# Four convolution layers on one core: the Fourier layer's modes kept with channels innermost, and the order of buffers at the start of layer 2

## The chip, the core and the metric

The kernel runs on one core of a Trainium2 chip. The core has TensorE (PE: matmuls; PEld: its weight loads), VectorE (DVE), ScalarE (ACT), GpSimd (POOL) and SyncE (SP, which here only issues transfers), a working memory SBUF of 128 partitions, the accumulators PSUM that matmuls write, and 16 DMA engines to the main memory. The metric is the device time of one execution in microseconds (us). A profile is one execution recorded instruction by instruction; its lines name the lines of the kernel file ("L1286" is line 1286).

The kernel is written in a language in which the programmer states operations on tiles, and the compiler adds the waits, picks buffers from pools and orders each engine's instructions. Inside a block `with tc.manual_schedule(...)` the order of the named engines is that of the text. Layers 0 to 2 have such a block around their main loop; layer 3 has none, nor have the lines ahead of the loop in layer 2.

## What is computed

The input x is 4 images of 64 channels and 256 x 256 points, all in 32-bit floats. Four layers follow one another; each adds to x a function of its group-normalized x:

```python
x = x + L0(gn(x))   # 1x1 conv, 8x8 patch FFT filter, depthwise 3x3, gated gelu, 1x1 conv
x = x + L1(gn(x))   # 3x3 conv
x = x + L2(gn(x))   # 3x3 neighbourhood differences select one of two 1x1 convs
x = x + L3(gn(x))   # Fourier layer

def gn(v, G=32, eps=1e-5):            # 32 groups of 2 channels, over a whole image
    return (v - mean) / sqrt(var + eps)

def L3(x, w1, w2):                    # M1 = M2 = 16 modes
    x_ft = rfft2(x)
    top = einsum('bixy,ioxy->boxy', x_ft[:, :, :16, :16], w1)
    bot = einsum('bixy,ioxy->boxy', x_ft[:, :, 256-16:, :16], w2)
    out_ft = zeros; out_ft[:, :, :16, :16] = top; out_ft[:, :, 256-16:, :16] = bot
    return irfft2(out_ft, s=(256, 256))
```

Only 32 x 16 of the Fourier modes are used, so layer 3 is done with small DFT matrices: along the rows' direction (h), then along w, then the product with the modes' weights, then back.

## The kernel before: the parts that the change touches

Three large buffers named slots are shared by all layers; each has two copies. A new tile in a slot takes the copy that becomes free:

```python
self.slots = tc.tile_pool(name="slot", bufs=2)
def slot(self, k, name):
    return self.slots.tile([128, 11, self.W + 2], F32, tag=f"y{k}", name=name)
```

Layer 1 loads its rows into slots 0 and 1 by turns (n is one of 64 steps), normalizes them on ScalarE into two tiles of slot 2, and has in its loop:

```python
xns = [self.slot(2, f"xn1_{k}")[:, 0:10] for k in range(2)]
...
x = xt[n] = self.slot(n % 2, f"x1_{n}")[:, 0:10, 0:W]        # load
...
for n in range(NI):                    # NI = 64, manual schedule
    load(n + 3)
    product(n, 1)                      # L852: matmuls
    fetch(n)                           # L860: ScalarE, s<-m
    product(n, 2)
    finish(n - 1)                      # ScalarE sums, store
    transform(n + 1, 1, 2)             # L842: VectorE, reads xn
    middle(n)                          # L866: VectorE, s<-s,m
    product(n, 0); result(n, 0)        # L872
    transform(n + 1, 0, 3)
    normalize(n + 2)                   # L256: ScalarE, xn<-x
    product(n, 3); result(n, 3)
```

Layer 2 begins with (L954 is the memset, L967 the load's transfer, L1004 that of r, L147 and L981 small constants):

```python
xns = [self.slot(k, f"xn2_{k}_{i}")[:, 0:10] for i, k in enumerate((1, 2, 2))]
z = p_z.tile([128, 2, 10, W + 2], F32, name="z")
for t in xns + [z[:, 0], z[:, 1]]:
    nc.gpsimd.memset(t[:, :, 0 : W + 2 : W1], 0.0)
...
def load(n, g, s, ins=None):           # step n, half g, side s
    if s == 0:
        xt[n, g] = self.slot(((2 * n + g) % 3) % 2, f"x2_{n}_{g}")[:, 0:10, 0:W]
    ... nc.sync.dma_start(...)
for n, g in ((0, 0), (0, 1), (1, 0)):
    for s in range(2):
        load(n, g, s)
...                                    # constants
with tc.manual_schedule(...):
    for g in range(2):
        normalize(0, g)                # L256: xn (2n+g) % 3 <- x (n, g)
    convolve(0)                        # L1082
    ...                                # L1038 differ, L1052 divergence
    load(1, 1, 0); load(1, 1, 1)
    load_r(0, 0, 0); ...
```

Layer 3, forward half. There are B = 4 images; a group is CC = 4 channels of one image, 1 MB, so 16 groups per image; x has six buffers (three slots of two). NW = NH = 2, M = 16, C = 64:

```python
for b in range(B):
    ah = p_ah.tile([128, NW, C, 4 * M], F32, tag="ah", name=f"ah_{b}")     # one buffer
    for c0 in range(0, C, CC):
        x = ...load(b, c0, ...)                            # L1217
        for c1 in range(0, CC, 4):
            ps = ps_a.tile([128, 2, W], F32, tag="a")      # two buffers
            for n in range(NH):
                for j in range(2):
                    nc.tensor.matmul(ps[halves[j]], eh[:, n, :],           # L1258: along h
                                     x[:, c1 + 2*j : c1 + 2*j + 2, n, :], ...)
            m = p_a.tile([128, 2, W], F32, tag="m")        # three buffers
            nc.scalar.copy(m, ps)                          # L1263
            pt = ps_t.tile([128, NW, 2, 2, 4 * M], F32, tag="t")           # two buffers
            for n in range(NW):
                for k in range(2):
                    nc.tensor.transpose(...pt[:, n, k]..., m[:, k, ...], self.ident)   # L1267
            for n in range(NW):
                nc.vector.tensor_copy(                     # L1273
                    ah[:, n, c : c + 4, :].rearrange("p (j k) f -> p k j f", j=2), pt[:, n])
    if b < 3:
        load_w(b * NK)                                     # 2 MB of weights

    psx = ps_x.tile([128, 4, 128], F32, tag="x")
    ahv = ah.rearrange("p n c (s g k r) -> p n g r k s c", s=2, g=4, k=4)
    for n in range(NW):
        for ri in range(2):
            for g in range(4):
                nc.tensor.matmul(psx[32*g : 32*g + 32]..., ew[:, n, ri, :], ahv[:, n, g, ri],
                                 ..., tile_position=(0, 32 * g))           # L1286: along w
    xw = p_a.tile([128, 4, 128], F32, tag="m")
    nc.scalar.copy(xw, psx)                                # L1293

    pxt = ps_x.tile([128, 2, 4, 4, 2, M], F32, tag="xt")
    for s in range(2):
        for k in range(4):
            for h in halves:
                nc.tensor.matmul(pxt[h, s, k]..., xw[:, k, s*C : (s+1)*C], self.ident, ...)   # L1299
    for s in range(2):
        xb = xm[:, s, :, :, :, b].rearrange("p (g k) w r -> p k g w r", g=4)
        for k in range(4):
            v = pxt[:, s, k].rearrange("p g r w -> p g w r")
            nc.vector.tensor_scalar(xb[up, k], v[up], r[up], None, ALU.mult)               # L1309
            nc.vector.tensor_scalar(xb[low, k, :, :, 0], v[low, :, :, 1], r[low], -1.0, ...)   # L1310
            nc.vector.tensor_scalar(xb[low, k, :, :, 1], v[low, :, :, 0], r[low], ...)      # L1311
    ...                                                    # L1314: two tiny operations
```

After the loop come the product with the modes' weights (L1325, tile psm, out of xm), and the inverse half (L1350 to L1384), which loads x again, adds the result and stores it. A 32-bit matmul is two instructions in the trace, a transpose one.

Of the kernel before, what the change touches and what calls it, by code (L numbers as in the profile page):

```python
# [10 lines left out]
F32 = mybir.dt.float32  # L11
U32 = mybir.dt.uint32
AF = mybir.ActivationFunctionType
ALU = mybir.AluOpType
# [3 lines left out]
C = 64  # L18
# [100 lines left out]
class _Net:  # L119
# [812 lines left out]
    def _layer2(self, ctx, src, dst):  # L932
        tc, nc, a, B, H, W = self.tc, self.nc, self.a, self.B, self.H, self.W
# [13 lines left out]
        W1 = W + 1  # L947
        halves = [slice(0, C), slice(C, 128)]
        quarters = [slice(k * Q, (k + 1) * Q) for k in range(4)]

        xns = [self.slot(k, f"xn2_{k}_{i}")[:, 0:10] for i, k in enumerate((1, 2, 2))]
        z = p_z.tile([128, 2, 10, W + 2], F32, name="z")
        for t in xns + [z[:, 0], z[:, 1]]:
            nc.gpsimd.memset(t[:, :, 0 : W + 2 : W1], 0.0)  # L954
        its = [(b, r0) for b in range(B) for r0 in range(0, H, 32)]
        NI = len(its)
        xt, xn, rt, q, masks, sels, po, bst = ({} for _ in range(8))

        def load(n, g, s, ins=None):
            if n >= NI:  # L960
                return
            b, r0 = its[n]
            if s == 0:
                xt[n, g] = self.slot(((2 * n + g) % 3) % 2, f"x2_{n}_{g}")[:, 0:10, 0:W]
            top = r0 + 16 * g + 8 * s - 1
            i0, i1 = max(0, -top), min(10, H - top)
            d = nc.sync.dma_start(xt[n, g][halves[s], i0:i1], src[b][:, top + i0 : top + i1, :])  # L967
            if ins:
                self.after(d, ins)

        for n, g in ((0, 0), (0, 1), (1, 0)):
            for s in range(2):
                load(n, g, s)
        ones = cp.tile([128, Q], F32, name="ones")
        nc.vector.memset(ones, 1.0)
        peri, thr, scl = self.load("peri", cp), self.load("thr", cp), self.load("scl", cp)
# [225 lines left out]
    def _layer3(self, ctx, src, dst):  # L1202
        tc, nc, a, B, H, W = self.tc, self.nc, self.a, self.B, self.H, self.W
        pool = lambda c, name, bufs, **k: c.enter_context(tc.tile_pool(name=name, bufs=bufs, **k))
        M = MODES
        NH, NW = H // 128, W // 128
        CC, NK = 4, 2
# [17 lines left out]
        eh = self.load("c_eh", cp)  # L1225
# [10 lines left out]
        with ExitStack() as c2:  # L1236
            p_w = pool(c2, "l3w", 3)
            p_ah, p_a = pool(c2, "l3ah", 1), pool(c2, "l3a", 3)
            ps_a, ps_t = pool(c2, "l3pa", 2, space=PSUM), pool(c2, "l3pt", 2, space=PSUM)
            ps_x, ps_m = pool(c2, "l3px", 1, space=PSUM), pool(c2, "l3pm", 1, space=PSUM)  # L1240
            wts, xs = {}, {}
            self.small = lambda name: ps_m.tile([128, 512], F32, tag="m", name=name)

            def load_w(k0):
                wt = wts[k0] = p_w.tile([128, 2, NK, M * C], F32, tag="w", name=f"wt_{k0}")
                nc.sync.dma_start(wt, a["wf"][:, :, k0 : k0 + NK])

            for b in range(B):

                ah = p_ah.tile([128, NW, C, 4 * M], F32, tag="ah", name=f"ah_{b}")  # L1250
                for c0 in range(0, C, CC):
                    x = first.pop(c0, None) if b == 0 else None
                    x = xs[b, c0] = x or load(b, c0, f"x3_{b}_{c0}")
                    for c1 in range(0, CC, 4):
                        ps = ps_a.tile([128, 2, W], F32, tag="a", name=f"psa_{b}_{c0}_{c1}")
                        for n in range(NH):
                            for j in range(2):
                                nc.tensor.matmul(  # L1258
                                    ps[halves[j]], eh[:, n, :], x[:, c1 + 2 * j : c1 + 2 * j + 2, n, :],
                                    start=(n == 0), stop=(n == NH - 1),  # L1260
                                )
                        m = p_a.tile([128, 2, W], F32, tag="m", name=f"a_{b}_{c0}_{c1}")
                        nc.scalar.copy(m, ps)  # L1263
                        pt = ps_t.tile([128, NW, 2, 2, 4 * M], F32, tag="t", name=f"psat_{b}_{c0}_{c1}")
                        for n in range(NW):
                            for k in range(2):
                                nc.tensor.transpose(  # L1267
                                    pt[:, n, k].rearrange("p j f -> p (j f)"),
                                    m[:, k, n * 128 : (n + 1) * 128], self.ident,
                                )  # L1270
                        c = c0 + c1
                        for n in range(NW):
                            nc.vector.tensor_copy(  # L1273
                                ah[:, n, c : c + 4, :].rearrange("p (j k) f -> p k j f", j=2), pt[:, n]
                            )
                    if c0 % 16 == 0:
                        self.next_norms()
                if b < 3:
                    load_w(b * NK)

                psx = ps_x.tile([128, 4, 128], F32, tag="x", name=f"psx_{b}")
                ahv = ah.rearrange("p n c (s g k r) -> p n g r k s c", s=2, g=4, k=4)
                for n in range(NW):
                    for ri in range(2):
                        for g in range(4):
                            nc.tensor.matmul(  # L1286
                                psx[32 * g : 32 * g + 32].rearrange("p k (s c) -> p k s c", s=2),
                                ew[:, n, ri, :], ahv[:, n, g, ri],
                                start=(n == 0 and ri == 0), stop=(n == NW - 1 and ri == 1),
                                tile_position=(0, 32 * g),  # L1290
                            )
                xw = p_a.tile([128, 4, 128], F32, tag="m", name=f"xw_{b}")
                nc.scalar.copy(xw, psx)  # L1293

                pxt = ps_x.tile([128, 2, 4, 4, 2, M], F32, tag="xt", name=f"psxt_{b}")
                for s in range(2):
                    for k in range(4):
                        for h in halves:
                            nc.tensor.matmul(  # L1299
                                pxt[h, s, k].rearrange("p g r w -> p (g r w)"), xw[:, k, s * C : (s + 1) * C],  # L1300
                                self.ident, start=True, stop=True,
                            )
                r, nb = self.r[3][:, b : b + 1], self.nb[3][:, b : b + 1]
                up, low = halves
                for s in range(2):
                    xb = xm[:, s, :, :, :, b].rearrange("p (g k) w r -> p k g w r", g=4)
                    for k in range(4):
                        v = pxt[:, s, k].rearrange("p g r w -> p g w r")
                        nc.vector.tensor_scalar(xb[up, k], v[up], r[up], None, ALU.mult)  # L1309
                        nc.vector.tensor_scalar(xb[low, k, :, :, 0], v[low, :, :, 1], r[low], -1.0, ALU.mult, ALU.mult)  # L1310
                        nc.vector.tensor_scalar(xb[low, k, :, :, 1], v[low, :, :, 0], r[low], None, ALU.mult)  # L1311
                for k, h in enumerate(halves):
                    dc = xm[h, 0, 0, 0, k, b : b + 1]
                    nc.vector.scalar_tensor_tensor(dc, nb[h], float(H * W), dc, ALU.mult, ALU.add)  # L1314

            for k0 in range(0, M, NK):
                if k0 + 2 * NK < M and k0 > 0:
                    load_w(k0 + 2 * NK)
                wt = wts[k0]
                ps = ps_a.tile([128, 2, W], F32, tag="a", name=f"psm_{k0}").rearrange("p k w -> p (k w)")  # L1320
                ps = ps[:, 0 : NK * M * 2 * B].rearrange("p (k w r b) -> p k w r b", k=NK, w=M, r=2)
                for k in range(NK):
                    for kw in range(M):
                        for s in range(2):
                            nc.tensor.matmul(  # L1325
                                ps[halves[s], k, kw].rearrange("p r b -> p (r b)"),
                                wt[:, s, k, kw * C : (kw + 1) * C],
                                xm[:, s, k0 + k, kw].rearrange("p r b -> p (r b)"), start=True, stop=True,
                            )
                for k in range(NK):  # L1330
                    nc.scalar.copy(om[:, :, :, 0:2, k0 + k], ps[:, k].rearrange("p w r b -> p w b r"))
                    nc.vector.tensor_scalar(om[:, :, :, 2, k0 + k], ps[:, k, :, 0, :], -1.0, None, ALU.mult)
# [84 lines left out]
```

## Time and profile before

The median of three runs is 7476.2 us (7473.46 to 7483.11). The profiled execution has a span of 7469.9 us and a mean granted TensorE clock of 0.97.

| engine | busy us | share of the span | instructions |
|---|---|---|---|
| PE | 7164.3 | 96% | 188280 |
| PEld | 4283.8 | 57% | 188280 |
| DVE | 6440.8 | 86% | 5705 |
| ACT | 3917.9 | 52% | 4173 |
| POOL | 658.6 | 9% | 1435 |

Layer 0 takes the span up to about 4830 us, layer 1 to about 5525, layer 2 to about 6830, layer 3 the rest, of which the forward half goes to 7093, the product with the modes' weights to 7149 and the inverse half to the end.

How to read the lines that follow. A line of groups gives engine, operation, what it writes and reads, shape and count; then busy time and the mean of one in ns; then the engine's idle time before it and what ended most of that. A line of waits reads "who <- on whom: total us, times, longest us". In a timeline, a line begins with its start and its length in us; successive instructions of a kind are merged (x8), so that an instruction's own length is not always to be seen; the bracket is the idle time before it. Matmuls overlap, so the mean of one matmul is longer than the distance from one to the next. The share of DMA is the mean busy share of the 16 DMA engines; it can come out slightly over 1.

### The profile page before, as it was taken

The numbers are of one execution on the slowest core, as the hardware profiler recorded it, in microseconds if no ns is written. First come the engines' busy times: TensorE is split into PE (matmuls) and PEld (weight loads), VectorE is DVE, ScalarE is ACT, GpSimd is POOL, SyncE is SP. The second block draws the span as 40 slices with busy tenths as digits, with TensorE's granted clock in tenths as the row PEclk, the third lists the DMA queues.
The fourth block names the chain that finished last, engine by engine and source line by source line (L and its number), as shares of the span: only waits on it lengthen the run. The fifth ranks groups of instructions, "written<-read, shape, count | busy, mean of one in ns | idle before, by whom it ended". The sixth has DMA issues, their size and how long they took to land. (4 is left out here: it accounts for less than half of the span.)

```text
span 7469.9 us, 396764 instructions
## 1 busy us (share of the span) xinstructions
PE 7164.3 (96%) x188280; PEld 4283.8 (57%) x188280; DVE 6440.8 (86%) x5705; ACT 3917.9 (52%) x4173; POOL 658.6 (9%) x1435
## 2 busy tenths in 40 slices
PE   6999999999999999999999999899989999998797
PEld 4666666666666666666666666533334444443275
DVE  7999999999999999999999999889979889885345
ACT  3444444444554444454445445377768877773111
POOL 0000000000000000000000000011102222221011
PEclk9999999999999999999999999999999999999955
DMA  3222222222222222222111111399967666667689
GB/s 131 63 64 63 62 63 61 59 63 62 60 62 60 60 63 63 60 61 57 46 46 47 47 46 48 76 223 228 229 149 181 172 178 175 172 173 235 239 350 393
DMA packets 651193, 875.49 MB, mean 117 GB/s; under 512 B 44020, under 2 KB 470212, under 8 KB 647524
## 3 DMA queue, kind: packets, MB, share of 16 engines
q1 hardware_dynamic: 568548, 581.61, 29.0%
q0 software_dynamic: 81024, 268.50, 12.4%
q8 instruction: 1477, 24.20, 1.4%
q14 instruction: 144, 1.18, 0.1%
HBM read 581.50 MB, written 268.44 MB: 114 GB/s over the span
## 5 line engine op out<-in xcount | busy, mean ns | idle before, releaser
L482 PE MATMUL psd<-y,diag 32*32 32x512 f32 x73296 | 2526.3, 597 | 8.0 <-issue 7.6
L520 DVE SCALAR_TENSOR_TENSOR v<-y,sb_w_dw,v 128x2048 f32<-128x2048 f32 x1024 | 2391.5, 2335 | 112.3 <-ACT v L518 89.3
L482 PEld LDWEIGHTS psd<-y,diag 32*32 32x32 f32 x73296 | 1534.6, 103 | 837.3 <-issue 309.9
L462 ACT COPY y<-psy 128x512 f32<-128x512 f32 x1536 | 916.8, 661 | 1671.0 <-PE psy L455 1669.6
L420 DVE TENSOR_TENSOR up<-psu,flt 128x768 f32<-128x768 f32 x1024 | 933.0, 952 | 210.0 <-PE psu L417 209.5
L455 PEld LDWEIGHTS psy<-sb_c_bdft,up 64*64 64x64 f32 x49152 | 855.2, 135 | 340.4 <-issue 127.0
L455 PE MATMUL psy<-sb_c_bdft,up 64*64 64x64 f32 x49152 | 925.0, 221 | 22.8 <-issue 19.5
L417 PE MATMUL psu<-win,xf 64*64 64x384 f32 x8192 | 788.5, 489 | 23.3 <-DVE h L502 10.5
L1038 DVE TENSOR_TENSOR q<-xn 128x2313 f32<-128x2313 f32 (+2 forms) x256 | 628.0, 2496 | 1.7 <-ACT xn L256 1.7
L1093 PE MATMUL one<-z,wp 32*32 32x512 f32 x16384 | 594.6, 597 | 17.6 <-issue 13.1
L1039 ACT ACTIVATE q<-q 128x2313 f32<-128x2313 f32 (+2 forms) x256 | 529.1, 2086 | 32.2 <-DVE q L1038 30.9
L496 ACT ACTIVATE h<-psd 128x1024 f32<-128x1024 f32 x258 | 250.6, 1023 | 516.4 <-PE psd L482 516.4
L256 ACT ACTIVATE xn<-x,nb,r 128x1024 f32<-128x1024 f32 (+3 forms) x272 | 487.1, 1794 | 28.3 <-DMA x<-x 24.4
L1093 PEld LDWEIGHTS one<-z,wp 32*32 32x32 f32 x16384 | 366.9, 103 | 226.4 <-issue 84.6
L1052 PE MATMUL div<-q,ones 64*32 64x512 f32 x8192 | 468.6, 598 | 13.7 <-ACT q L1039 9.8
L427 POOL MEMSET y<- 128x22 f32 x384 | 51.8, 136 | 4212.2 <-ACT y L435 3204.1
L417 PEld LDWEIGHTS psu<-win,xf 64*64 64x64 f32 x8192 | 302.3, 135 | 193.1 <-issue 88.7
L1126 POOL DMA_DIRECT2D x<-r x512 | 273.5, 541 | 971.4 <-DVE r L1123 880.9
L852 PE MATMUL m<-t,wk 64*64 64x512 f32 x3072 | 341.1, 588 | 0.0
L1052 PEld LDWEIGHTS div<-q,ones 64*32 64x32 f32 x8192 | 154.1, 107 | 321.8 <-issue 257.8
L535 DVE TENSOR_TENSOR v<-g,v 64x1024 f32<-64x1024 f32 x257 | 313.5, 1220 | 9.3 <-ACT g L528 1.4
L502 DVE TENSOR_TENSOR h<-h,psd 128x1024 f32<-128x1024 f32 x258 | 302.7, 1215 | 6.1 <-PE psd L482 5.7
(154 smaller groups left out, 7403.2 us busy)
## 6 DMA issues: line engine op xcount, KB each, us to landing
x<-x SPq DMA_DIRECT2D x240, 640.0 KB, 6.6
x<-x SPq DMA_DIRECT2D x122, 1024.0 KB, 10.5
x<-in_x_dram SPq DMA_DIRECT2D x256, 256.0 KB, 3.7
x<-o POOLq DMA_DIRECT2D x128, 512.0 KB, 8.0
r<-x SPq DMA_DIRECT2D x512, 128.0 KB, 4.0
x<-r POOLq DMA_DIRECT2D x512, 128.0 KB, 3.8
out_dram<-x POOLq DMA_DIRECT2D x64, 1024.0 KB, 10.0
r<-in_x_dram SPq DMA_DIRECT2D x248, 256.0 KB, 3.8
```

The costliest lines, as they stand in the source:

```text
L256: self.nc.scalar.activation(dst, src, AF.Identity, bias=self.nb[n][p0:p1, b : b + 1], scale=self.r[n][p0:p1, b : b + 1])
L417: nc.tensor.matmul(ps[halves[n], s, 0:384], xf[t][halves[s], n, 4 * g + k], win[halves[s]], start=True, stop=True)
L420: nc.vector.tensor_mul(ups[t, g][:, :, k, :], ps[:, :, 0:384], flt.broadcast_to([128, 2, 384]))
L455: nc.tensor.matmul(ps[halves[c], n, s, :, k, :], up[halves[n], s, k, i * 128 + c * C : i * 128 + (c + 1) * C], bdft[halves[n]], start=True ...
L462: nc.scalar.copy(yt[t][i][:, 3:11, w0 : w0 + 64].rearrange("p r (k n w) -> p n r k w", k=4, n=2), ps[:, :, s])
L482: ins = nc.tensor.matmul(d[q // 2][quarters[j], q % 2], diag[quarters[q], i, k, :], rows_in(t, i, quarters[q], j, dy)[:, :, dx : dx + W], ...
L520: nc.vector.scalar_tensor_tensor(v, s, wdw[:, 2, k : k + 1], v, ALU.mult, ALU.add)
L852: nc.tensor.matmul(rows2(m)[halves[j], s], w[dx][halves[s]], ts[n][halves[s], i, 2 * j : 2 * j + 2, dx : dx + W], start=(dx == 0), stop=(d ...
L1038: nc.vector.tensor_sub(d, p0, p1)
L1039: nc.scalar.activation(d, d, AF.Square)
L1052: ins = nc.tensor.matmul(ps[quarters[j], h], ones[halves[h]], q[n, g, k][halves[h], r + 2 * j : r + 2 * j + 2, o : o + W], start=(m == 0), ...
L1093: ins = nc.tensor.matmul(rows2(ps[g])[quarters[j], k], w[quarters[i]], z[quarters[i], h, 2 * j + dy : 2 * j + dy + 2, dx : dx + W], tile_p ...
```

## The change

In layer 2 the first three loads are written ahead of the xn tiles, and xn takes its first two tiles from slot 2 and the third from slot 1; before, it took slot 1 first, and ahead of the loads. It is meant to give the first loads their buffers earlier.

In layer 3 the tile ah keeps the channels innermost, so that the matmuls along w read neighbours; PSUM tile pxt is laid out so that one VectorE operation covers all sixteen rows of modes, which makes 6 operations of 24 per image. The loop is written as steps over all 64 groups: step i has the matmuls of group i and the transposes of group i − 1, and an image's work along w follows one step after its last group.

```diff
-        xns = [self.slot(k, f"xn2_{k}_{i}")[:, 0:10] for i, k in enumerate((1, 2, 2))]
         z = p_z.tile([128, 2, 10, W + 2], F32, name="z")
-        for t in xns + [z[:, 0], z[:, 1]]:
-            nc.gpsimd.memset(t[:, :, 0 : W + 2 : W1], 0.0)
 ...
         for n, g in ((0, 0), (0, 1), (1, 0)):
             for s in range(2):
                 load(n, g, s)
+        xns = [self.slot(k, f"xn2_{i}")[:, 0:10] for i, k in enumerate((2, 2, 1))]
+        for t in xns + [z[:, 0], z[:, 1]]:
+            nc.gpsimd.memset(t[:, :, 0 : W + 2 : W1], 0.0)
 ... (layer 3)
+            ah_of = lambda b: ahs[b].rearrange("p n (s g k r) c -> p n g r k s c", s=2, g=4, k=4)
+            def along_h(b, c0):     # load, the matmuls of psa, ScalarE's copy: as before
+            def turned(b, c0):
+                if c0 == 0:
+                    ahs[b] = p_ah.tile([128, NW, 4 * M, C], F32, tag="ah", name=f"ah_{b}")
 ...                                  # the transposes as before
-                            nc.vector.tensor_copy(
-                                ah[:, n, c : c + 4, :].rearrange("p (j k) f -> p k j f", j=2), pt[:, n]
-                            )
+                    nc.vector.tensor_copy(
+                        ahs[b][:, n, :, c0 : c0 + 4].rearrange("p f (j k) -> p k j f", j=2), pt[:, n]
+                    )
+            def along_w(b):         # the matmuls of psx and ScalarE's copy, out of ah_of(b)
+            def spread(b):
-                pxt = ps_x.tile([128, 2, 4, 4, 2, M], F32, tag="xt", name=f"psxt_{b}")
+                pxt = ps_x.tile([128, 2, 4, 4, 2 * M], F32, tag="xt", name=f"psxt_{b}")
-                                pxt[h, s, k].rearrange("p g r w -> p (g r w)"), xw[:, k, s * C : (s + 1) * C],
-                                self.ident, start=True, stop=True,
+                                pxt[h, s, :, k], xw[:, k, s * C : (s + 1) * C], self.ident, start=True, stop=True
 ...
-                    xb = xm[:, s, :, :, :, b].rearrange("p (g k) w r -> p k g w r", g=4)
-                    for k in range(4):
-                        v = pxt[:, s, k].rearrange("p g r w -> p g w r")
-                        nc.vector.tensor_scalar(xb[up, k], v[up], r[up], None, ALU.mult)
-                        nc.vector.tensor_scalar(xb[low, k, :, :, 0], v[low, :, :, 1], r[low], -1.0, ALU.mult, ALU.mult)
-                        nc.vector.tensor_scalar(xb[low, k, :, :, 1], v[low, :, :, 0], r[low], None, ALU.mult)
+                    xb = xm[:, s, :, :, :, b]
+                    v = pxt[:, s].rearrange("p g k (r w) -> p (g k) w r", r=2)
+                    nc.vector.tensor_scalar(xb[up], v[up], r[up], None, ALU.mult)
+                    nc.vector.tensor_scalar(xb[low, :, :, 0], v[low, :, :, 1], r[low], -1.0, ALU.mult, ALU.mult)
+                    nc.vector.tensor_scalar(xb[low, :, :, 1], v[low, :, :, 0], r[low], None, ALU.mult)
 ...
+            groups = [(b, c0) for b in range(B) for c0 in range(0, C, CC)]
+            for i in range(len(groups) + 2):
+                if i < len(groups):
+                    along_h(*groups[i])
+                b, k = divmod(i - 1, NG)              # NG = 16 groups per image
+                if b > 0 and k == 0:
+                    along_w(b - 1)
+                if 0 < i <= len(groups):
+                    turned(*groups[i - 1])
+                if b > 0 and k == 0:
+                    spread(b - 1)
+                if i % NG == NG - 1 and i // NG < 3:
+                    load_w(i // NG * NK)
```

## The prediction

> **What bounds the kernel now.** I read the page first: TensorE is busy 96% of the span, so the time is TensorE's time plus its waits. The change touches two stretches only: the passage from layer 1 to layer 2 and the forward half of layer 3. So I asked each stretch for its own waits, groups and timeline.
>
> The passage, timeline between 5481 and 5512 us (start, length, engine, line, what; in brackets the idle time before it and who ended it):
>
> ```profile
> 5481.46 13.15 SPq L1004 DMA_DIRECT2D r<-x  x8
> ...
> 5487.58 2.79 ACT L256 ACTIVATE xn<-x,nb,r 64x256 f32<-64x256 f32 x2
> ...
> 5494.72 3.99 SPq L967 DMA_DIRECT2D x<-x  x2
> ...
> 5506.49 2.52 ACT L256 ACTIVATE xn<-x,nb,r 128x2560 f32<-128x2560 f32 x1 [16.12 <-DMA x<-x]
> 5508.92 1.09 ACT L860 ACTIVATE s<-m,i 128x1024 f32<-128x1024 f32 x1
> ...
> 5510.06 1.99 PE L852 MATMUL m<-t,wg 64*64 64x512 f32 x8 [9.57 <-ACT s L860]
> ```
>
> The ACTIVATE at 5506.49 is layer 2's: it normalizes rows (0,1), which the DMA of L967 fetches. That load was issued only at 5494.72, behind eight loads of r. ScalarE stands still for 16.12 us, and behind it in ScalarE's queue is L860, which belongs to layer 1. So TensorE idles 9.57 us inside layer 1.
>
> Why is the load late? Before takes layer 2's first xn from slot 1. Slot 1 has two buffers: the first one to fall free goes to xn (memset at 5469.54), the second is held by layer 1's last x until its normalization at 5487.58 has run its 2.79 us, to 5490.4.
>
> Layer 3, forward. The groups and waits between 6826 and 7100 us (groups: busy us, mean ns; then idle before; waits: total, times, longest):
>
> ```profile
> L1258 PE MATMUL psa<-x,sb_c_eh 128*64 128x512 f32 x512 | 130.1, 619 | 3.4 <-DVE r L1123 3.4
> L1273 DVE COPY ah<-psat 128x256 f32<-128x256 f32 x128 | 47.9, 420 | 131.2 <-PE psat L1267 130.9
> L1286 PE MATMUL psx<-ah,ew 128*32 128x512 f32 x128 | 28.2, 1034 | 1.0 <-DVE ah L1273 1.0
> L1309 DVE TENSOR_SCALAR xm<-psxt,r 64x128 f32<-64x128 f32 x32 | 14.2, 445 | 39.6 <-PE psxt L1299 39.1
> L1310 DVE TENSOR_SCALAR xm<-psxt,r 64x64 f32<-64x64 f32 x32 | 10.9, 340 | 0.5
> ```
> ```profile
> PE psat L1267 <- ACT a L1263: 42.9, 57, 1.8
> PE psm L1325 <- DVE xm L1314: 8.6, 1, 8.6
> ```
>
> Two things to see: psx streams 512 columns like psa, but takes 1034 ns against 619; and the transposes wait for ScalarE's copy in 57 of 64 groups. A steady group, from the timeline:
>
> ```profile
> 6851.72 0.66 PE L1267 MATMUL psat<-sb_c_ident,a 128*128 128x128 f32 x4 [0.72 <-ACT a L1263]
> 6852.31 1.94 PE L1258 MATMUL psa<-x,sb_c_eh 128*64 128x512 f32 x8
> 6854.33 0.58 ACT L1263 COPY a<-psa 128x512 f32<-128x512 f32 x1 [2.66 <-PE psa L1258]
> 6854.97 0.66 PE L1267 MATMUL psat<-sb_c_ident,a 128*128 128x128 f32 x4 [0.72 <-ACT a L1263]
> ```
>
> One group is 6854.97 − 6851.72 = 3.25 us. Last, windows of equal kind (length, busy of PE, PEld, DVE, ACT, POOL with counts, then granted clock, DMA share, GB/s):
>
> ```profile
> 6972.00:7011.00 39.00, 30.16 (x147) 11.26 (x146) 9.97 (x27) 7.02 (x12) 0.00 (x0) 1.00 1.02 362
> 7093.00:7149.00 56.00, 54.79 (x1024) 54.73 (x1024) 4.00 (x16) 6.04 (x16) 0.00 (x0) 0.50 0.49 190
> 7149.00:7470.00 321.00, 266.03 (x1408) 204.07 (x1408) 179.85 (x289) 38.68 (x64) 48.22 (x64) 0.56 1.01 399
> ```
>
> In the first the DMA engines are already full at 362 GB/s. The last two, the product with the modes' weights and the inverse half, are not edited; the inverse half is full of transfers (share 1.01).
>
> [...] psx reads elements 64 floats apart (256 bytes) and takes 1034 ns for 512 columns; psa reads neighbours and takes 619. [...] the trace has 0.50 all through the modes' product, which follows 8.6 us of waiting.
>
> **The change, part by part.**
>
> 1. Layer 2's first loads. Load (0,1) now gets the buffer of slot 1 that is free at 5469.5, and xn takes slot 2 for its first two tiles. The load can then land long before layer 1's tail needs ScalarE. The new waits are that xn tiles 0 and 1 need layer 1's own xn buffers: the trace shows the memset of the first at 5491.34, right after layer 1's VectorE work on it. They are waits on VectorE, not on a queue of transfers. I take back TensorE's 9.57 us, and nothing more, since everything after it in the passage hangs on layer 1's end: **−9.6 us**.
>
> 2. psx. With channels innermost its 64 channels are neighbours. Its 32 instructions run in four column groups, so eight steps; the trace has 7.06 us for them, 0.86 us a step. psa, with neighbours, has steps of 0.43 us (weight loads at 6856.03 and 6856.46). So 3.4 us, four times, all on TensorE: 4 × 3.5 = **−14 us**.
>
> 3. The 24 VectorE operations become 6. Before, the last run takes from 7084.49 to 7092.57, 8.1 us. From the two sizes in the groups the slope is (445 − 340)/64 = 1.64 ns per element; so 512 elements take 445 + 384 × 1.64 = 1075 ns and 256 take 340 + 192 × 1.64 = 655 ns. Two times (1075 + 2 × 655) = 4.8 us. Only the last of the four is on the path, the wait of psm: **−3.3 us**.
>
> 4. VectorE's copies into ah pay for it: their output now steps 256 bytes. Before shows what such a step costs elsewhere: ScalarE's L1373 takes 0.60 us for 256 elements with a stepped output, L1263 0.58 us for 512 without. [...] VectorE has 3.25 us per group: hidden, **0**.
>
> 5. The loop. Transposes of group i−1 are now written after the matmuls of group i, so ScalarE's copy could hide behind them. TensorE's own work for a group is 4 × 0.43 = 1.71 us plus 0.58 us of transposes = 2.29, so 0.96 us is to be had per group, 62 us at most. Two things cut it. First, transfers: a group is 1.05 MB, at 362 GB/s 2.90 us. Second, the layout of instructions. Layer 3 has no manual schedule, and the trace shows that the compiler reorders: after the first spread it placed 20 matmuls of psa (two and a half groups) between two sets of transposes (timeline at 6907.49), and at 6844.10 it placed ten, two of them of the next group. So matmuls that are ready move ahead of transposes, and transposes that are ready should likewise move ahead of matmuls whose x is not there. Up to group 37 the runs of matmuls straddle groups, and from 6981 on they do not: the compiler then took x to be late. In the new loop TensorE gets through its groups sooner, so the six loads in advance run out sooner. I guess the new order holds for some 15 groups and for a few after each of three spreads beyond those that already ran ahead, 20 in all: 20 × 0.96 = **−19 us**.
>
> 6. The modes' product and the inverse half: no edit, **0**. Weights are loaded three times in the forward half as before.
>
> Sum: −9.6 − 14 − 3.3 − 19 = −45.9, so 7476.2 − 45.9 = **7430.3 us**.
>
> **The rivals.** (a) The order is undone: the compiler puts each transpose straight after its copy as before. For: 57 waits of 64 in a kernel whose matmuls were free to move. Against: in the new text the matmuls stand first. Then only parts 1 to 3 count, −27, **7449 us**. (b) The order holds throughout and transfers take over as the bound. 58 groups of 1.05 MB and three weights of 2.1 MB are loaded in the forward half, 67 MB, of which about 6 are there by 6848 (18 us at 386 GB/s in that window, layer 2's last stores among them); 61 MB at 362 GB/s are 169 us, so the last x lands near 7017; about 13 us of transposes, psx and spread follow, and psm begins at 7030 instead of 7093. With part 1: −73, **7403 us**. (c) The wait of part 1 only moves: ScalarE now waits for slot 2 in the middle of layer 1. For: the first two xn do come later than before. Against: 5491 is still before the gap. It would take back up to 10 us: 7440. (d) The stepped copies become the bound of layer 3. They would have to exceed 1.6 us each, against 0.42 now: I give it almost nothing; it would cost about what the rest brings.
>
> **Range and chances.** (b) and (a) set the ends, widened by 5 us for the passage and for runs (7473 to 7483): 7398 to 7460. A gain of over 2% would need 150 us; all of layer 3's forward half is 263, and transfers keep 170 of it. A loss of 2% has no mechanism here that is large enough. Faster by over 2%: 0.02; within 2%: 0.97; slower: 0.01.
>
> **What would show it.** Right: no ScalarE wait on a transfer near 5490 to 5506 and TensorE without a gap there; psx near 600 ns; six TENSOR_SCALAR of 64x512 and 64x256 per batch near 1.1 and 0.65 us; the wait of psat on ScalarE down from 57 times to about 40. Wrong: psx still near 1 us (then the step was not the cause); copies into ah above 1.5 us; a forward half with the DMA share near 1 from end to end (then rival b); the inverse half longer, or its clock changed, which I hold fixed.

## The result, and the profile after

The changed kernel takes 7434.57 us (median, 7423.01 to 7437.48); the kernel before, in turns on the same chip, 7478.82 us. The ratio is 0.9938, 95% interval 0.9921 to 0.9956: 44 us less, where 45.9 were predicted.

Single profiled executions differ by more than a step is worth in stretches that nobody edited: layer 0, the same code in the same order, takes from 4837 to 4875 us in the profiles of this case. So each step is read in its own stretch, from starts and ends of matmuls in the trace. Stretches repeat better than totals: layer 3's forward half, where it is as before, takes 263.0 to 264.0 us in four profiles.

| stretch, us | before | after |
|---|---|---|
| layer 1, first to last matmul of m | 675.5 | 664.4 |
| gap of TensorE from there to the first psz of layer 2 | 10.4 | 10.6 |
| layer 2, first psz to first psa | 1297.8 | 1293.2 |
| layer 3 forward, first psa to first psm | 263.0 | 228.4 |
| psm to the end | 376.9 | 377.7 |

Two stretches carry the gain, 11.1 and 34.6 us. First the passage, timeline of the changed kernel (L964 is the load of x, L973 the memset of xn):

```profile
5480.55 26.49 SPq L964 DMA_DIRECT2D x<-x  x6
...
5502.29 0.13 POOL L973 MEMSET xn<- 128x20 f32 x1 [0.64 <-DVE t L842]
...
5502.46 2.94 ACT L256 ACTIVATE xn<-x,nb,r 64x256 f32<-64x256 f32 x2 [1.05 <-POOL xn L973]
...
5507.08 11.55 SPq L1004 DMA_DIRECT2D r<-x  x8
...
5512.75 2.52 ACT L256 ACTIVATE xn<-x,nb,r 128x2560 f32<-128x2560 f32 x1 [2.33 <-POOL xn L973]
```

The loads of x now stand ahead of the eight loads of r; before, the load of rows (0,1) stood behind them. ScalarE's two normalizations wait 1.05 and 2.33 us for the memset of their buffer, no longer 16.12 us for a transfer, and TensorE has no gap in layer 1.

Then layer 3, forward half: TensorE's waits, and the groups.

```profile
PE psat L1274 <- ACT a L1264: 27.6, 40, 2.0
...
PE psm L1346 <- DVE xm L1319: 5.2, 1, 5.2
```
```profile
L1278 DVE COPY ah<-psat 128x256 f32<-128x256 f32 x128 | 66.1, 601 | 120.4 <-PE psat L1274 120.3
...
L1290 PE MATMUL psx<-ah,ew 128*32 128x512 f32 x128 | 16.6, 597 | 1.4 <-DVE ah L1278 1.4
...
L1314 DVE TENSOR_SCALAR xm<-psxt,r 64x512 f32<-64x512 f32 x8 | 9.2, 1152 | 10.4 <-PE psxt L1306 10.3
```

psx has gone from 1034 to 597 ns a matmul and from 28.2 to 16.6 us in all, the copies into ah have gone from 420 to 601 ns, and the transposes wait for ScalarE in 40 groups instead of 57. Two of the four psx are not done in one go: the compiler puts the matmuls of a group's psa between their first 10 and their last 22 instructions, and such a psx takes 1.90 + 2.77 us, an undivided one 3.64:

```profile
6878.30 1.90 PE L1290 MATMUL psx<-ah,ew 128*32 128x512 f32 x10
...
6882.00 2.77 PE L1290 MATMUL psx<-ah,ew 128*32 128x512 f32 x22
...
6985.69 3.64 PE L1290 MATMUL psx<-ah,ew 128*32 128x512 f32 x32 [0.68 <-DVE ah L1278]
```

Timeline of the transposes, with the matmuls of psa left out: where the new order holds, a group takes 2.45 us (6847.24 − 6844.79); later in the same image the compiler puts a group's transposes right behind its copy again, and a group takes 3.27 us (6875.85 less 6872.58):

```profile
6844.79 0.66 PE L1274 MATMUL psat<-sb_c_ident,a 128*128 128x128 f32 x4
...
6847.24 0.66 PE L1274 MATMUL psat<-sb_c_ident,a 128*128 128x128 f32 x4
...
6872.58 0.66 PE L1274 MATMUL psat<-sb_c_ident,a 128*128 128x128 f32 x4 [0.16 <-ACT a L1264]
...
6875.85 0.66 PE L1274 MATMUL psat<-sb_c_ident,a 128*128 128x128 f32 x4 [0.74 <-ACT a L1264]
```

Windows: the first 30 us of steady work, the modes' product, and the inverse half. The last two are as before.

```profile
6842.00:6872.00 30.00, 30.00 (x148) 11.06 (x147) 12.60 (x24) 7.09 (x13) 0.00 (x0) 1.00 1.03 382
...
7054.00:7110.00 56.00, 54.79 (x1024) 54.70 (x1024) 4.05 (x16) 6.04 (x16) 0.00 (x0) 0.50 0.50 190
7110.00:7431.00 321.00, 269.12 (x1408) 208.12 (x1408) 180.00 (x289) 38.77 (x64) 48.24 (x64) 0.54 1.01 399
```

### The profile page after: what moved, and what is told of

It is laid out like the page before. It is cut to its first block, busy times and chain, and to the rows that moved or that the text cites. A ratio compares the mean times of both kernels' runs of the same rounds, so it can differ in the third digit from the quotient of the medians.

```text
span 7431.7 us, 396686 instructions
## 1 busy us (share of the span) xinstructions
PE 7153.8 (96%) x188280; PEld 4277.8 (58%) x188280; DVE 6445.5 (87%) x5633; ACT 3918.2 (53%) x4173; POOL 659.2 (9%) x1435
## 3 DMA queue, kind: packets, MB, share of 16 engines
q1 hardware_dynamic: 568548, 581.61, 29.3%
## 5 line engine op out<-in xcount | busy, mean ns | idle before, releaser
L417 PE MATMUL psu<-win,xf 64*64 64x384 f32 x8192 | 785.7, 488 | 22.3 <-DVE h L502 10.4
L1093 PE MATMUL one<-z,wp 32*32 32x512 f32 x16384 | 594.7, 599 | 15.5 <-issue 11.4
L256 ACT ACTIVATE xn<-x,nb,r 128x1024 f32<-128x1024 f32 (+3 forms) x272 | 487.1, 1794 | 15.3 <-DMA x<-x 8.3
```

The lines of the kernel that those rows point to most:

```text
L256: self.nc.scalar.activation(dst, src, AF.Identity, bias=self.nb[n][p0:p1, b : b + 1], scale=self.r[n][p0:p1, b : b + 1])
L417: nc.tensor.matmul(ps[halves[n], s, 0:384], xf[t][halves[s], n, 4 * g + k], win[halves[s]], start=True, stop=True)
L1093: ins = nc.tensor.matmul(rows2(ps[g])[quarters[j], k], w[quarters[i]], z[quarters[i], h, 2 * j + dy : 2 * j + dy + 2, dx : dx + W], tile_p ...
```

## The experiments

The theory: the passage gives 10 us, psx its own time, the spread's end 3 us, and the order of the loop the rest, in so far as the compiler keeps it. The rivals: the order counts for nothing, or transfers set the pace. A ratio below is to the kernel before on the same chip; "forward" is the stretch from the first psa to the first psm.

### One part alone: layer 2

```diff
 (before)
-        xns = [... for i, k in enumerate((1, 2, 2))]     # and their memsets, ahead of the loads
         ... the first three loads ...
+        xns = [... for i, k in enumerate((2, 2, 1))]     # and their memsets
```

> Before with the edit of layer 2 alone. If the gain there comes from the early load, layer 1 (first matmul on tile m to the last) shortens from 668 us by 9.6 to 11 us, TensorE's wait on ScalarE's s inside it is gone, and layer 3 stays as before (263 us from the first psa to the first psm). If the wait only moved to slot 2, layer 1 keeps a gap of 5 us or more and shortens by less than 5. Whole kernel about 10 us less; layer 0 is not edited, so a different layer 0 is run-to-run spread.

Measured: 7462.26 us, ratio 0.9976 (0.9966 to 0.9987). Layer 1's stretch falls from 675.5 to 665.1 us; forward is 263.4 us, as before. The wait was worth 10.4 us and is independent of layer 3.

### One part alone: the layout, in the loop of before

```diff
 (before)
-                ah = p_ah.tile([128, NW, C, 4 * M], F32, ...)
+                ah = p_ah.tile([128, NW, 4 * M, C], F32, ...)
-                    24 operations per image into xm
+                    6 operations per image into xm
```

> Before with the layout alone: channels innermost in ah, 6 VectorE operations of 24, the old order of the loop, layer 2 as before. My theory: the parts add, so the forward half of layer 3 shrinks from 263 us by 4 x 3.5 for psx and 3.3 for the last spread, to about 246; the wait of the transposes on ScalarE stays at 57 of 64. Rival: the layout made the loop overlap (VectorE gets free sooner), then it falls to 235 or less and the loop alone gives little.

Measured: 7457.2 us, ratio 0.9974 (0.9963 to 0.9985), forward 251.6 us: −11.4. An image's psx takes 3.64 us instead of 7.06, 13.7 for four, and the wait of psm 5.2 instead of 8.6. That would be 17, but the compiler orders the rest anew, and TensorE's waits now read:

```profile
PE psat L1267 <- ACT a L1263: 44.7, 61, 0.7
...
PE psat L1267 <- DMA x<-x: 3.2, 1, 3.2
```

That is 1.8 us more on ScalarE, and 3.2 us on a transfer at the start of layer 3 that before does not have. All of TensorE's waits in the stretch together are 1.2 us longer than before, in spite of the shorter wait of psm; with psx that makes −12.5 us, and TensorE's other matmuls take the 1.1 us more that are missing to −11.4. Near 246 us had been expected.

### One part alone: the loop, with the layout of before

```diff
 (the changed kernel)
-                    ahs[b] = p_ah.tile([128, NW, 4 * M, C], F32, ...)
+                    ahs[b] = p_ah.tile([128, NW, C, 4 * M], F32, ...)    # and 24 operations per image
 (and layer 2 as before)
```

> The new loop alone, with the old layout of ah, 24 VectorE operations, layer 2 as before. My theory: about 18 us off the forward half of layer 3 (263 to 245), psx still near 1030 ns, the wait on ScalarE down to about 40 of 64. Rival: the loop needs the shorter psx and spread to run ahead; then it gives under 8 us by itself.

Measured: 7466.01 us, ratio 0.9977 (0.9967 to 0.9988), forward 253.8 us: −9.2, between the theory's −18 and the rival's −8. The waits on ScalarE fall by 20.1 us, more than in the whole change, but other waits appear:

```profile
PE psat L1274 <- ACT a L1264: 22.8, 33, 1.0
...
PE psat L1274 <- DVE ah L1278: 5.3, 3, 2.7
```
```profile
L1290 PE MATMUL psx<-ah,ew 128*32 128x512 f32 x128 | 31.9, 1033 | 1.0 <-DVE ah L1278 1.0
```
```profile
7012.00:7022.00 10.00, 7.11 (x31) 2.19 (x27) 7.58 (x24) 1.39 (x3) 0.00 (x0) 0.90 0.84 297
7022.00:7032.00 10.00, 8.52 (x41) 3.23 (x39) 2.93 (x8) 1.75 (x3) 0.00 (x0) 0.93 0.80 259
```

With 2.8 us on transfers and the rest, TensorE's waits account for −13.8 us. Two things take part of it back. psx needs 31.9 us for 28.2, +3.7, because here too two of the four are cut by a group's psa. And around and after the last wait on VectorE the granted clock is 0.90 and 0.93 over 10 us each (the last two lines, windows; the clock stands third from the end), where it is 1.00 in the windows before and behind: from 7019.26 to 7023.99 TensorE takes 4.73 us for work of 3.05 (a group of 2.45 and four more transposes of 0.6), +1.7. That makes −8.4 of the −9.2. The parts don't add: −11.4 and −9.2 make −20.6, and together they bring −34.6. The wait of psat on VectorE's copies, 5.3 us here and absent with the new layout, is one reason, and the lower clock that was measured after it is another; the next experiments show both by themselves. The waits for a transfer, 3.2 us with the layout and 2.8 here, belong to neither part: the kernel with layer 2 alone has one of 2.5.

### The order held

```diff
 (the changed kernel)
+            with tc.manual_schedule(engines={mybir.EngineType.PE}):
                 for i in range(len(groups) + 2):
                     ... the loop, indented ...
```

> The changed kernel with TensorE's order in the forward loop of layer 3 held to that of the text, nothing else. If the compiler's order is what leaves 40 waits, these go, a group takes 2.45 us throughout while transfers keep up, and the forward half falls from 228 us to between 190 (TensorE's pace alone) and 203 (61 MB at 362 GB/s and the end): 25 to 38 us less than the changed kernel, with TensorE now waiting for x in some groups. Rival: the transfers are already the bound in the second stretch of 3.26 us (DMA share 0.99 there); then holding the order gives less than 8 us and the waits on ScalarE turn into waits on x.

Measured: 7398.43 us, ratio 0.989 (0.9876 to 0.9905), forward 199.1 us: 29.3 below the changed kernel, with the same instructions. Waits, and windows:

```profile
PE psat L1274 <- DMA x<-x: 7.7, 1, 7.7
...
PE psat L1274 <- ACT a L1264: 0.2, 1, 0.2
```
```profile
6842.00:6872.00 30.00, 29.89 (x152) 11.93 (x151) 13.35 (x32) 6.68 (x13) 1.09 (x2) 1.00 1.04 397
6890.00:6920.00 30.00, 30.00 (x149) 11.15 (x148) 14.74 (x30) 7.14 (x13) 0.00 (x0) 1.00 1.05 393
```

In these windows TensorE is busy in 29.89 and 30.00 of 30 us and the DMA engines are full too, at 397 and 393 GB/s (379 from 6930 to 6960): the two limits lie together, and x comes in time. All four psx are undivided. So the compiler's own order, not the transfers, kept the changed kernel at 228 us. The same kernel on another chip, with this expectation:

> The held order once more, beside the version with the early constants on the same chip. Ratio to before 0.989 as the first time, 0.9875 to 0.9905; forward half 197 to 202 us, gap at the start of layer 2 10.5 us.

gave 7406.38 us, ratio 0.9891 (0.9874 to 0.9907), forward 198.9 us, gap at the start of layer 2 10.4 us.

### The order held, with the old layout, and with the old loop

```diff
 (the order held)
-ahs[b] = p_ah.tile([128, NW, 4 * M, C], F32, ...)      # first: 24 operations and the old layout
+ahs[b] = p_ah.tile([128, NW, C, 4 * M], F32, ...)
 (the order held)
-for i in range(len(groups) + 2): ...                   # second: the loop of before,
+for b in range(B): for c0 in range(0, C, CC): ...      # the new layout
```

> The loop of the changed kernel with TensorE's order held, and the changed layer 2, but ah and pxt in the layout of before (24 VectorE operations, psx with a step of 256 bytes). Beside the held order with the new layout (forward half 199.1 us from the first psa to the first psm). Theory 'the gain of the layout is TensorE's own time and shows in full once the order is held': psx 1035 ns, 4 x 3.5 us more of psx and 3 to 7 us more in the last spread, forward half 213 to 222 us, total near 7415. Rival 'transfers set the pace, so psx hides behind them': only the last image's psx and spread show, forward half 203 to 209 us, total near 7404.

Measured: 7442.41 us, ratio 0.9934 (0.9915 to 0.9952), forward 228.4 us: 29.3 above the held order with the new layout, more than even the theory's upper end, and not hidden behind transfers. After an image's end, timeline of this kernel:

```profile
6959.94 2.32 DVE L1278 COPY ah<-psat 128x256 f32<-128x256 f32 x6
...
6960.84 0.63 PE L1274 MATMUL psat<-sb_c_ident,a 128*128 128x128 f32 x4 [2.80 <-DVE ah L1278]
```

and at the same place with the new layout:

```profile
6936.12 1.94 DVE L1278 COPY ah<-psat 128x256 f32<-128x256 f32 x4
...
6937.54 0.66 PE L1274 MATMUL psat<-sb_c_ident,a 128*128 128x128 f32 x4
```

The copies come after the 24 operations in VectorE's queue. These keep it from 6951.47 to 6959.94, 8.5 us, so the copies queue up (six in a row), both buffers of psat stay full, and TensorE waits 2.80 us; the six operations take 5.1 us (6931.04 to 6936.12) and end early enough. Such a wait comes at three boundaries, 8.4 us. After the first and the third TensorE's matmuls take nearly twice as long for a while:

```profile
6908.10 0.63 PE L1274 MATMUL psat<-sb_c_ident,a 128*128 128x128 f32 x4 [2.80 <-DVE ah L1278]
6908.66 3.61 PE L1259 MATMUL psa<-x,sb_c_eh 128*64 128x512 f32 x8
...
7011.91 1.09 PE L1274 MATMUL psat<-sb_c_ident,a 128*128 128x128 f32 x4 [2.81 <-DVE ah L1278]
...
7012.93 3.68 PE L1259 MATMUL psa<-x,sb_c_eh 128*64 128x512 f32 x8
```

Eight matmuls take 3.61 and 3.68 us for 1.94. At the first boundary a group takes 4.10 us for 2.45, at the third two groups up to 7019.64 take 7.73 us for 4.90: 1.7 and 2.8 us lost. With psx (13.7) and the last spread (3.4) that is 30.0 us; other waits are 0.5 us shorter, which leaves 29.5 for the 29.3 measured.

Not so after the second boundary, where the eight matmuls from 6961.40 on take 1.94 us. Windows of 10 us around each boundary, and the one after the third (PE's busy time stands second, the granted clock third from the end):

```profile
6904.00:6914.00 10.00, 7.20 (x30) 2.18 (x26) 6.02 (x19) 1.17 (x2) 0.00 (x0) 0.83 0.79 262
...
6954.00:6964.00 10.00, 7.20 (x38) 2.66 (x36) 7.97 (x26) 1.73 (x3) 0.00 (x0) 1.00 0.92 312
...
7004.00:7014.00 10.00, 7.19 (x34) 2.98 (x34) 8.96 (x29) 1.76 (x3) 0.00 (x0) 0.86 0.84 284
7014.00:7024.00 10.00, 10.00 (x42) 3.42 (x40) 2.27 (x6) 1.76 (x3) 0.00 (x0) 0.80 0.71 230
```

The three waits are equally long and TensorE is equally busy around them (7.20, 7.20 and 7.19 us), but the clock is 0.83 at the first, 1.00 at the second, and 0.86 and then 0.80 at the third. Why the second boundary keeps its clock is not shown.

> The new layout and the changed layer 2, but the loop of before (each group's transposes right after its copy, each image's psx and spread before the next image), with TensorE's order held as written. Theory 'ScalarE's copy on the path of every group is what the loop is about': 64 waits of psat on ScalarE of 0.72 us or more, 3.26 us per group, 64 x 3.26 = 209 us, and four psx and spreads of 8 to 11 us that nothing overlaps, forward half 240 to 252 us, total 7440 to 7450. Rival 'it is holding the order as such that brings the gain, whatever the order': forward half near 200 us.

Measured: 7476.61 us, ratio 0.9975 (0.9968 to 0.9982), forward 254.6 us, 55.5 above the new loop and 2.6 above the theory's range; one wait for a transfer at the layer's start takes 9.6 us. The line of waits on ScalarE is

```profile
PE psat L1268 <- ACT a L1264: 46.9, 63, 1.0
```

Holding an order brings nothing by itself (in the compiler's own order this loop takes 251.6 us); what is held must keep ScalarE's copy off TensorE's path.

### How many neighbours the matmul needs

```diff
 (the changed kernel; R = 4, then R = 2)
-ahs[b] = p_ah.tile([128, NW, 4 * M, C], F32, ...)
+ahs[b] = p_ah.tile([128, NW, C // R, 4 * M, R], F32, ...)   # psx: 16 steps of 256 columns for 8 of 512
```

> The changed kernel with ah cut so that 4 channels (16 bytes) are neighbours, and psx in 16 steps of 256 columns for 8 of 512. Theory [...] psx takes 3.4 us per image as with 64 neighbours; VectorE's copies [...] stay at 600 ns. Rival 'every step other than to the neighbour costs' : psx near 7 us per image. Rival 'it is the width of the step, 256 bytes': copies fall from 601 to about 420 ns. Total within 15 us of the changed kernel.

> The same with 2 channels (8 bytes) as neighbours. [...] psx between 3.4 us [...] and 5 us per image; copies [...] take between 420 and 600 ns. Rival 'every step costs': psx near 7 us. Total within 15 us of the changed kernel.

Measured: 7451.78 and 7439.52 us (one execution each; the kernel before takes 7497.27 on that chip), forward 228.2 and 229.0 us, as in the changed kernel. Groups, R = 4 first:

```profile
L1278 DVE COPY ah<-psat 128x256 f32<-128x256 f32 x128 | 68.6, 625 | 117.8 <-PE psat L1274 117.7
...
L1289 PE MATMUL psx<-ah,ew 128*32 128x256 f32 x256 | 15.9, 381 | 1.4 <-DVE ah L1278 1.4
```
```profile
L1278 DVE COPY ah<-psat 128x256 f32<-128x256 f32 x128 | 48.1, 420 | 137.4 <-PE psat L1274 137.2
...
L1289 PE MATMUL psx<-ah,ew 128*32 128x256 f32 x256 | 16.0, 381 | 1.0 <-DVE ah L1278 1.0
```

Both layouts give TensorE its full pace (an undivided psx takes 3.66 and 3.70 us, against 3.64). VectorE writes single numbers 16 bytes apart as slowly as 256 bytes apart (625 and 601 ns), and single numbers 8 bytes apart at the old 420 ns. So both rivals fell: psx with fours or pairs as neighbours is nowhere near 7 us, and a step of 16 bytes in place of 256 brings the copies nothing.

### Layer 2: which half of the edit does it

```diff
 (before; first run)
-        ... xn's tiles and memsets, then the first three loads
+        ... the first three loads, then xn's tiles and memsets      # slots 1, 2, 2
 (before; second run)
-        xns = [... for i, k in enumerate((1, 2, 2))]
+        xns = [... for i, k in enumerate((2, 2, 1))]                # still ahead of the loads
```

> Before, with the first three loads of layer 2 written ahead of the xn tiles, but xn taking slots 1, 2, 2 as before. Theory 'what matters is that the load of rows (0,1) gets the buffer of slot 1 that is free early': the wait of ScalarE for that transfer (16.12 us) and TensorE's gap of 9.6 us go as with the whole edit, and the first xn's memset moves to about the time of layer 1's last normalization plus its length, without a wait longer than 3 us on ScalarE. Rival 'the slots of xn matter as well': the first normalization waits for that memset, ScalarE stands still, and 3 us or more of the gap of TensorE stay.

> Before, with xn taking slots 2, 2, 1, but still written ahead of the loads. Theory as above: the third xn takes the early buffer of slot 1, the load of rows (0,1) still waits for the second, TensorE's gap of 9.6 us stays. Rival 'the slots alone are enough': the gap goes.

Measured: 7476.18 and 7468.74 us (one execution each; before takes 7488.08 on that chip); layer 1's stretch is 663.8 and 664.2 us. Either half takes the gap away, so the expectation of the second run fell. In that run, layer 1's last normalization runs from 5500.34 to 5503.13; then come this load and, later, layer 2's second normalization:

```profile
5503.15 1.26 SPq L967 DMA_DIRECT2D x<-x  x2
```
```profile
5514.54 2.53 ACT L256 ACTIVATE xn<-x,nb,r 128x2560 f32<-128x2560 f32 x1 [2.32 <-POOL xn L954]
```

By its slot the load is that of (0,1): as expected, it goes out only at 5503.15, when layer 1's last x has been read. But the early buffer of slot 1 now goes to the third xn and not to the first, so layer 2's first two normalizations stand later in ScalarE's order (5504.27 and 5514.54; before, the first ran at 5469.71 already and the second stood in front of an L860 that TensorE needed), and the load isn't kept behind those of r. When the second one's turn comes, it waits for its xn and no longer for x. In the first run and in the changed kernel the two normalizations stand later as well (from 5505.40 on; 5502.46 and 5512.75). The cause was thus a normalization placed early in ScalarE's queue whose x came late. In the second run it is the later place that mends most of it: counted from the end of layer 1's last normalization the load goes out only 4.3 us earlier than before, and ScalarE had waited 16.12 us. Whether an earlier x would mend it with the early place kept, no run here shows.

### A version that is faster than both

```diff
 (the order held)
-        cp, p_q = pool("l2c", 1), pool("l2q", 5)
+        cp, p_q = self.cp, pool("l2q", 5)          # the pool of constants that lives all through
```

> The held order, and layer 2's small constants in the pool that lives all through, so that their transfers need not wait until layer 1's pools are given back (before and after, TensorE has 10.3 to 10.6 us without work there, which ends with nthr and wc). Theory 'the constants' transfers are the path': the first psz waits for layer 1's last evacuation instead (5521.90 + 1.23 in the changed kernel) and starts some 8 us earlier; of these 6 to 9 us stay, as the differences on VectorE, which wait for layer 1's last ScalarE work, come next. Total 5 to 9 us below the held order on the same chip. Rival 'the gap ends with the release of layer 1's other pools anyway': a gap of 9 to 10 us stays and the total is the same.

Measured: 7389.93 us, ratio 0.9869 (0.9854 to 0.9883); the held order beside it 0.9891. The gap at the start of layer 2, in the changed kernel and in this one:

```profile
5532.42 7.36 PE L1082 MATMUL psz<-xn,wc 64*64 64x512 f32 x40 [10.59 <-DVE nthr L978]
```
```profile
5509.50 3.66 PE L1082 MATMUL psz<-xn,wc 64*64 64x512 f32 x32 [1.44 <-DVE o L872]
```

9.0 us of 10.4 are gone; forward is 200.4 us and layer 2 from psz on 1292.8 us, as with the held order (198.9 and 1294.5). The medians lie 16.5 us apart, more than the 5 to 9 expected, and only 9.0 of it is shown to come from the edit: of the 23.3 us between the two profiled executions 15.8 lie ahead of layer 1, where nothing was edited.

## Why the prediction was right

What TensorE's matmuls and waits took in layer 3's forward half (busy 204.1 us before and 190.9 after, waits for the rest) makes up its stretch:

| | before | after | difference | predicted |
|---|---|---|---|---|
| four psx | 28.2 | 16.6 | −11.6 | −14 |
| psat waits for ScalarE | 42.9 | 27.6 | −15.3 | −19 |
| psm waits for the last spread | 8.6 | 5.2 | −3.4 | −3.3 |
| TensorE's smaller waits | 7.3 | 4.6 | −2.7 | 0 |
| TensorE's other matmuls | 175.9 | 174.3 | −1.6 | 0 |
| the stretch | 263.0 | 228.4 | −34.6 | −36.3 |

1. **Layer 2's first loads**: −9.6 predicted, −11.1 in the profiles (−10.4 with this part alone), and the waits named in advance, on the memsets of xn, are there with 1.05 and 2.33 us. The reason was half right: the early buffer was to be the cure, but every run without the gap also has the normalization later in ScalarE's order, and the run with the slots alone shows that this place does most of it.
2. **psx**: the cause right, the sum too large. An undivided psx takes 3.64 us against an estimate of 3.4, but the compiler cut two of the four, 4.67 us each, so that the four bring 11.6 us and not 14.
3. **Six operations for 24**: 1152, 690 and 660 ns against estimates of 1075 and 655; −3.4 against −3.3. "Only the last of the four is on the path" was too narrow. In the order that the changed loop aims at, each earlier spread of 24 operations stops TensorE for 2.8 us, and in two of three cases the clock was lower besides (0.83 and 0.86 in the windows above, 1.00 in the other). It did no harm to the sum here, since in the compiler's order of before such waits come to 1.2 us.
4. **Copies into ah**: 601 ns for 420; hidden, as said: with R = 2, at 420 ns, forward is no shorter (229.0 us).
5. **The loop**: 20 groups were guessed; the waits fell from 57 to 40, that is 17, and by 15.3 us for 19. The count of about 40 waits came out exactly, and the shape too: 13 groups in a row in the first image, where "some 15" were guessed, then five, five and one at the three image boundaries. But the guess had no strong ground: what the compiler would keep was not to be read from the profile of before. Why it falls back is not shown either; that it takes x to be late, no run varied.
6. **The modes' product and the inverse half**: 376.9 and 377.7 us, the clock at 0.50 and about 0.55: 0, right.

That 44 us come so near to 45.9 is in part luck: psx and the loop bring 6.1 us less than was put on them, and layer 2, the smaller waits and the other matmuls 5.8 us more. That the parts were added up was right for the sum and wrong as a rule: alone, the layout and the loop bring 20.6 of 34.6 us. Rival (b), 7403 us, is what the loop would have brought if its order had been kept: the held order took 7398.43. Its forward half was put at 200 us (7030 less 6830) and took 199.1. The rate of 362 GB/s under it was too low, 379 to 397 were reached; TensorE's own pace of 2.45 us per group is as near a bound. Rival (a) is ruled out by the 40 waits, (c) by layer 1's stretch, (d) by R = 2.

Left open: why two parts of 20.6 us become 34.6 together, beyond the waits and the clock named above; and the wait of 7.7 us for the first transposes of the held order, which no experiment took away.

## What to carry to other kernels

A rewritten loop is worth what the compiler's order leaves of it: look up in the timeline whether the new order stands, and hold it where it doesn't, for here this was worth nearly as much again as the edit of layer 3's forward half (29.3 us beside 34.6). A block of work that stands between two steps of a pipeline in an engine's queue (24 small operations, a normalization whose input is late) costs what the buffers behind it can't take up (8.5 us on VectorE stopped TensorE for 2.8 us, 5.1 us not at all), so shorten it or place it later. And where one engine writes what another reads, a layout with pairs as neighbours may suit both (here 3.70 us for a psx and 420 ns for a copy).

## What the runs showed of the hardware

- The matmuls along w, in 32-bit numbers, read pairs 8 bytes wide as fast as 64 neighbours, but single numbers 256 bytes apart at half the pace (3.70, 3.64 and 7.06 us for a psx).
- VectorE's copy of 256 numbers out of PSUM took 420 ns with a step of 4 (neighbours) or 8 bytes in its output, and 601 to 625 ns with one of 16 or 256.
- With TensorE's order held and the old layout, TensorE waits 2.80, 2.80 and 2.81 us at three image boundaries. The granted clock in the 10 us around them is 0.83, 1.00 and 0.86, and the next eight matmuls of psa take 3.61, 1.94 and 3.68 us.
- In the modes' product the granted clock is 0.50 over 56 us, although TensorE is busy for 54.79 us of them.
